# A message-passing layer on one core: picked rows put together by TensorE, slots in PSUM, ranks straight from TensorE's counts

## The chip, the cores and the metric

One of the 8 cores of a Trainium2 chip runs the whole program. The metric is the device time of one execution in microseconds (us). Engines are named as in the profile: PE (TensorE), DVE (VectorE), ACT (ScalarE), POOL (GpSimd) and SP (SyncE, which issues most DMAs).

## The reference

A graph layer over N = 6250 nodes and E = 206250 edges, 64 features, float32. The edges are sorted by their target `dst`.

```python
h = jnp.maximum(_layernorm(x, axis=-1), 0.0)
msg = jax.nn.relu(h[src] + edge_attr)
agg = jax.ops.segment_sum(msg, dst, num_segments=x.shape[0])
h = h + agg
h = jax.nn.relu(h @ W1 + b1)
out = x + h @ W2 + b2
```

So each edge needs one row of h out of 6250 (a gather by `src`), an addition of its attribute, a relu, and a sum into its target's row.

## The kernel before

**Layout.** Edges are taken in 269 groups of 768 (128 partitions x G = 6 columns; the last is short). `z` in SBUF holds h transposed and collects the sums: one-hot matmuls (`window_sum`) sum a group's messages into a window of W = 32 nodes, and DVE adds the window into `z` at the group's first node (`sum_into_z`). `slot` holds each edge's place in its window, and `one_hot` compares it with the numbers 1 to 32 (`slots`).

**Rows come in two ways.** Of each column of 128 edges the 128 rows of h are either gathered by POOL from `h_rows` in DRAM (an indirect DMA for one column, `gather`, each with a memset of the small tile `rest` behind it on POOL's queue), or picked on chip by PE. After the first F0 = 5 groups, the groups come in sets (`GROUPS`, KS = 144 sets): five of every six sets hold two groups, three columns of each gathered and three picked; the sixth holds one group, with all six columns picked. So a set has 6 or 0 gathers, and always 6 picked columns.

**Picking.** h lies in `hp` as two float16 parts, high and low, of every node. For a pair of sets (d), DVE compares node numbers with `sources` (`find`, four compares of 1536 columns, giving `found`; two ACT operations, `find_begin` and `find_beyond`, do the last 49th of the nodes) and ranks with `spots` (`back`, six compares of 1536, giving `backs`). PE multiplies `hp` by `found` (`across_of`), turns it (`turn_of`), and multiplies `picked` by `backs` into a PSUM pick bank (`pick`). The numbers that the compares look for (rank, part, spot) are worked out for 18 columns at a time in the `rank_*` steps: PE counts, before each edge, the earlier edges of the same part (`rank_count`), and DVE takes the rank out of these counts (`rank_of`).

**Decoding.** The pick bank holds for each column a high part and a low part, and a value that is one last bit smaller than its two parts say is stored negated: the value is max(b, -ONE_LESS * b) with b = high + low/FINE. In `decode(k)` ACT scales the low part (L685), DVE adds (L687), takes the maximum (L689), adds the edge attribute (L692), and adds the attributes of the gathered columns too (L695, which waits for the set's gathers). `messages` is ACT's relu (L702).

**Order.** The schedule is manual: each engine runs its instructions in the order in which the code records them. `both_units(k)` is one unit, for one set: first DVE's part (decode of set k-1, the compares for the pairs ahead, the rank steps, the one-hot of set k-1, the adds into z of set k-3), with the steps woven together by `weave`; then three stages s = 0, 1, 2 of PE and ACT: a turn, an across, in one of them the messages or the window sums of set k-2, and two of the unit's six picked columns. POOL's gathers for a set wait for picks of the set AHEAD = 9 earlier (`fetch_next`), and a ring of 11 buffers holds what they bring.

Of the kernel before, what the change touches and what calls it, by code (L numbers as in the profile page):

```python
# [68 lines left out]
BIAS, STEP = 4096, 512  # L69
# [4 lines left out]
ONE_LESS = 1 - 2.0 ** -24  # L74
# [6 lines left out]
def kernel(  # L81
# [77 lines left out]
    nc.gpsimd.iota(from0, pattern=[[1, S], [0, H]], base=0, channel_multiplier=0, allow_small_or_imprecise_dtypes=True)  # L159
# [8 lines left out]
    nc.vector.memset(ones_b, 1.0)  # L168
    upper = const.tile([P, P], F16, name="upper")
# [3 lines left out]
    for j in range(J):  # L173
        nc.gpsimd.iota(ids[j * S:(j + 1) * S], pattern=[[STEP * J, Q]], base=BIAS + STEP * j,
                       channel_multiplier=1, allow_small_or_imprecise_dtypes=True)
# [146 lines left out]
    ats, counts, marks, holds, ranks, spot_i = {}, {}, {}, {}, {}, {}  # L322
# [5 lines left out]
    def rank_count(c):  # L328
        ps = psum.tile([P, RG, PARTS, H], F32, name="rows", bufs=1)
        at = ats[c]  # L330
        nc.tensor.matmul(ps, upper, at, start=True, stop=False)
        for d in range(1, H):
            last = nc.tensor.matmul(ps[:, :, :, d:], ones_b, at[:, :, :, :H - d], start=False, stop=(d == H - 1))
# [4 lines left out]
    def rank_counted(c):  # L338
        counts[c] = rank.tile([P, RG, PARTS, H], F16, name="before", bufs=1)
        nc.scalar.copy(counts[c], made.pop(c))  # L340

    def rank_of(c):
        mine = counts.pop(c)
        nc.vector.tensor_tensor(mine, mine, ats[c], ALU.mult)
        yield
        ranks[c] = rank.tile([P, CC], F16, name="rank_of")
        with nc.allow_low_precision("a rank is a whole number below 2048"):
            nc.vector.tensor_reduce(ranks[c].rearrange("p (g j) -> p g j", j=H),
                                    mine.rearrange("p g m j -> p g j m"), AX.X, ALU.add)
# [20 lines left out]
    def rank_fits(c):  # L370
        rk = ranks.pop(c).rearrange("p (g j) -> p g j", j=H)
        pieces = ((0, 2, G - H), (2, 4, 0), (4, RG, G - H)) if c % 2 == 0 else ((0, RG, G - H),)
        for u, to, c0 in pieces:
# [5 lines left out]
            nc.vector.scalar_tensor_tensor(mine, rk[:, u:to], float(S), mine, op0=ALU.is_lt, op1=ALU.mult)  # L379
# [43 lines left out]
    pick_banks = [psum.tile([P, 2, 512], F32, name=f"pick{i}", bufs=1) for i in range(2)]  # L423
    turns = [pick_banks[0][:, 0], pick_banks[0][:, 1], half_banks[1], half_banks[2]]
    turns_made = [0]

# [49 lines left out]
    def ln_parts(r, m, h):  # L476
# [13 lines left out]
        nc.vector.tensor_tensor(hp[:, r:r + m], hp[:, r:r + m], sign.unsqueeze(2).to_broadcast([PP, m, 2, D]), ALU.mult)  # L490
# [68 lines left out]
    beyond = const.tile([P, 1], F32, name="beyond")  # L559
    nc.vector.tensor_scalar_mul(beyond, nodes_of[:, BB:], -1.0)  # L560

    def find_begin(d):
        found[d] = hot.tile([P, PARTS * BB + J, 4, S], F16, name="found")
        far = found[d][:, BB * PARTS:].rearrange("p m u s -> p (m u s)")
        nc.scalar.activation(far, sources[d][:, :J * 4 * S], AF.Abs, bias=beyond)
        return far

    def find_beyond(far):
        nc.scalar.activation(far, far, AF.Relu, bias=ones[:, 0:1], scale=-1.0)

    def find(d):
# [52 lines left out]
    def pick(k, i, t):  # L624
        d, u = k // 2, k % 2 * 2 + i
        ps = pick_banks[k % 2][:, i, :2 * H * D].rearrange("p (w t d) -> p w t d", w=2, t=H)
# [30 lines left out]
    def one_hot(gs):  # L657
        n = len(gs) * G
        g = gs[0]
        oh = work.tile([P, 2 * G, W], F32, name="oh", bufs=2)  # L660
        it = nc.vector.tensor_tensor(
            oh[:, :n], slot[:, g * G:g * G + n].unsqueeze(2).to_broadcast([P, n, W]),
            slots.unsqueeze(1).to_broadcast([P, n, W]), ALU.is_equal)
# [14 lines left out]

    def decode(k):
        ps = pick_banks[k % 2][:, :, :2 * H * D].rearrange("p i (w s) -> p i w s", w=2)  # L680
        n = len(GROUPS[k])
        ea, xg = eas[(k + RAWS) % EAS][:, :n], xgs[(k + RAWS) % RING]
        h = ps[:, :, 0]
        both = work.tile([P, 2, H * D], F32, name="both", bufs=1)
        nc.scalar.mul(both, ps[:, :, 1], 1.0 / FINE)  # L685
        yield
        nc.vector.tensor_tensor(both, h, both, ALU.add)  # L687
        yield
        nc.vector.scalar_tensor_tensor(h, both, -ONE_LESS, both, op0=ALU.mult, op1=ALU.max)  # L689
        yield  # L690
# [479 lines left out]
```

## Time and profile before

| | |
|---|---|
| time, median of 3 runs | 1239.59 us (1237.26 to 1239.94) |
| profiled execution | 1239.42 us, span 1237.4 us, mean granted clock 0.897 |
| PE, DVE, ACT, POOL busy | 918.2, 1005.9, 804.4, 1089.7 us |
| gathers and memsets on POOL | 748 each, 768.7 and 320.6 us |

A row of a group reads: line, engine, operation, out<-in, shapes, count | busy us, mean ns | idle us just before, and what ended it. A row of the timeline reads: start, us, engine, line, operation, count, and in brackets idle time before. A row of the waits reads: engine and line <- what it waited for: us in total, times, longest. A row of the stages reads: from:to, length, busy us and (count) of each engine, granted clock, DMA share, GB/s.

### The profile page before, as it was taken

How to read it: one execution, taken by the hardware profiler on the slowest of the kernel's cores; microseconds unless marked ns; L12 is line 12 of the kernel's file. 1: busy time of each engine (PE TensorE's matmuls, PEld its weight loads, DVE VectorE, ACT ScalarE, POOL GpSimd, SP SyncE). 2: the span in 40 equal slices, each digit the busy share in tenths (PEclk: the TensorE clock that was granted, in tenths of full speed). 3: DMA queues.
4: the chain of work that ended last, by engine and by line, in shares of the span. 5: the costliest groups of instructions: out<-in, count | busy, mean ns of one | idle time of the engine just before them, and what ended most of it. 6: DMA issues, size and time to landing. Idle time of an engine off the chain costs nothing. (4 is left out here: it accounts for less than half of the span.)

```text
span 1237.4 us, 37614 instructions
## 1 busy us (share of the span) xinstructions
PE 918.2 (74%) x14441; PEld 840.1 (68%) x14441; DVE 1005.9 (81%) x2286; ACT 804.4 (65%) x1605; POOL 1089.7 (88%) x1511
## 2 busy tenths in 40 slices
PE   1348888889877868858778768777886886787864
PEld 0227887778766867758767767777775785776754
DVE  8778999999887878868878877887787797786764
ACT  4438778778756757748657656676675775675642
POOL 8888988889888988988888888888888888888884
PEclk9969999999988889979889888898888988998977
DMA  6315565555554435535445445454554554454531
GB/s 194 96 41 168 168 184 156 169 174 160 152 145 147 148 107 153 154 112 166 138 143 155 135 118 147 138 159 129 147 150 134 162 150 121 135 154 123 159 73 49
DMA packets 92788, 173.63 MB, mean 140 GB/s; under 512 B 23673, under 2 KB 61178, under 8 KB 92602
## 3 DMA queue, kind: packets, MB, share of 16 engines
q1 hardware_dynamic: 68554, 146.58, 36.2%
q0 software_dynamic: 23936, 24.56, 11.3%
q8 instruction: 115, 1.88, 0.6%
q14 instruction: 71, 0.58, 0.1%
q10 hardware_dynamic: 112, 0.03, 0.0%
HBM read 167.22 MB, written 3.87 MB: 138 GB/s over the span
## 5 line engine op out<-in xcount | busy, mean ns | idle before, releaser
L225 POOL DMA_INDIRECT xg<-h_rows,src_sb x718 | 736.4, 1026 | 127.3 <-issue 77.4
L628 PE MATMUL pick<-picked,backs 128*128 128x128 f16 x5184 | 403.6, 234 | 1.2 <-DVE z L655 1.2
L622 ACT CAST picked<-half 128x512 f16<-128x512 f32 x432 | 253.2, 586 | 155.8 <-PE half L614 150.7
L628 PEld LDWEIGHTS <-backs 128*128 128x128 f16 x5184 | 338.3, 105 | 16.8 <-issue 7.1
L228 POOL MEMSET rest_of_pool<- 128x256 f16 x748 | 320.6, 429 | 0.4
L604 PE MATMUL half<-found,hp 128*128 128x128 f16 x3456 | 290.9, 232 | 27.2 <-ACT picked L622 25.8
L584 DVE TENSOR_SCALAR backs<-spots,ids 128x1536 f16<-128x1536 int16 x432 | 284.8, 686 | 0.1
L609 ACT CAST across<-half 128x512 f16<-128x512 f32 x432 | 258.3, 598 | 31.8 <-PE half L604 25.7
L604 PEld LDWEIGHTS <-hp 128*128 128x128 f16 x3456 | 240.8, 106 | 43.8 <-issue 36.6
L695 DVE SCALAR_TENSOR_TENSOR ea<-xg,ea 128x384 f32<-128x384 f32 x120 | 66.5, 554 | 158.0 <-DMA xg<-h_rows,src_sb 130.7
L574 DVE TENSOR_SCALAR found<-sources,nodes_of 128x1536 f16<-128x1536 int16 x288 | 188.3, 694 | 6.2 <-PE pick L628 4.1
L614 PE MATMUL half<-ident_h,across 128*128 128x128 f16 x1728 | 183.2, 233 | 0.8 <-ACT across L609 0.8
L702 ACT ACTIVATE ea<-ea 128x768 f32<-128x768 f32 x144 | 115.6, 803 | 100.8 <-DVE ea L695 95.6
L716 PE MATMUL pick<-oh,ea 128*64 128x32 f32 x3224 | 127.6, 229 | 8.8 <-ACT ea L702 8.8
L716 PEld LDWEIGHTS pick<-oh,ea 128*64 128x64 f32 x3224 | 111.0, 143 | 34.0 <-issue 15.7
L614 PEld LDWEIGHTS <-across 128*128 128x128 f16 x1728 | 127.9, 106 | 1.4 <-ACT across L609 1.2
L685 ACT ACTIVATE both<-pick 128x384 f32<-128x384 f32 x144 | 70.6, 490 | 50.8 <-PE pick L628 42.8
L687 DVE TENSOR_TENSOR both<-pick,both 128x384 f32<-128x384 f32 x144 | 78.1, 542 | 30.7 <-ACT both L685 29.8
L402 PE MATMUL rows<-holds,marks 128*96 128x96 f16 x288 | 28.0, 238 | 95.9 <-DVE holds L366 89.7
L384 PE MATMUL rows<-ident_b,spot_i 128*18 128x128 bf16 x48 | 11.6, 241 | 117.1 <-DVE spot_i L352 116.9
L402 PEld LDWEIGHTS <-marks 128*96 128x96 f16 x288 | 26.5, 152 | 97.1 <-DVE marks L362 77.6
L384 PEld LDWEIGHTS <-spot_i 128*18 128x18 bf16 x48 | 4.2, 88 | 125.6 <-DVE spot_i L352 124.2
(124 smaller groups left out, 914.3 us busy)
## 6 DMA issues: line engine op xcount, KB each, us to landing
sources<-source_row SPq DMA_DIRECT2D x72, 768.0 KB
ea<-in_edge_attr_dram SPq DMA_DIRECT2D x118, 384.0 KB
spots<-spot_rows SPq DMA_DIRECT2D x72, 384.0 KB
xg<-h_rows,src_sb POOLq DMA_INDIRECT x718
ea<-in_edge_attr_dram SPq DMA_DIRECT2D x32, 192.0 KB
xb<-in_x_dram SPq DMA_DIRECT2D x12, 128.0 KB
out_dram<-o SPq DMA_DIRECT2D x12, 128.0 KB
h_rows<-x SPq DMA_DIRECT2D x3, 384.0 KB
```

The source lines that it names most:

```text
L225: it = nc.gpsimd.indirect_dma_start(out=xg[:, j, :], out_offset=None, in_=rows[:, :], in_offset=bass.IndirectOffsetOnAxis(ap=idx[:, j:j + ...
L228: nc.gpsimd.memset(rest, 0.0)
L574: nc.vector.tensor_scalar(found[d][:, b * PARTS + m:b * PARTS + m + PARTS // 2].rearrange("p m u s -> p (m u s)"), sources[d][:, m * 4 * S ...
L584: nc.vector.tensor_scalar(backs[d][:, q, w].rearrange("p t s -> p (t s)"), spots[d].bitcast(I16), ids[:, w * QW + q:w * QW + q + 1], None, ...
L604: last = nc.tensor.matmul(ps[:, j * P:(j + 1) * P], hp[:, b * PARTS + m].rearrange("p t d -> p (t d)"), found[d][:, b * PARTS + m].rearran ...
L609: nc.scalar.copy(across[d, q].rearrange("p u j s -> p j u s"), ps.rearrange("p (j u s) -> p j u s", j=J, u=4))
L614: last = nc.tensor.matmul(ps[:, u * P:(u + 1) * P], ac[:, u].rearrange("p j s -> p (j s)"), ident_h, start=True, stop=True)
L622: nc.scalar.copy(picked[d][:, q].rearrange("p u d -> p (u d)"), turned.pop((d, q)))
L628: it = nc.tensor.matmul(ps[:, :, t], backs[d][:, q % QW, q // QW, u * H + t, :], picked[d][:, q, u].rearrange("p (w d) -> p w d", w=2), st ...
L687: nc.vector.tensor_tensor(both, h, both, ALU.add)
L702: nc.scalar.activation(msg, msg, AF.Relu)
L716: last = nc.tensor.matmul(pa[i * D:(i + 1) * D], msg[:, j, :], oh[:, j, :], start=(j < lo + 2), stop=(j >= G - 2))
```

## The change

1. **Decode by PE.** ACT copies a half of a pick bank to SBUF as float16 (`both`) and makes relu(-high) (`minus`); PE adds four products with scaled identities (`weigh_high`, `ident_h`, `weigh_sign`, `weigh_last`) back into the same bank; DVE then needs one addition per half, straight from PSUM. L687 and L689 go. In `ln_parts` only the high part takes the sign.
2. **Slots in PSUM.** `one_hot` reads the numbers 1 to 32 from a spare corner of a pick bank instead of SBUF.
3. **Ranks off the counts.** PE adds AMONG = 1024 where an edge has its own part (`ahead_h`), so that DVE takes the rank by a maximum straight from PSUM; the copy to SBUF (`rank_counted`, L340) and the product with `at` (L344) go. Numbers that ranks are compared with are shifted by 1024.
4. **The third compare on DVE.** `find_begin` and `find_beyond` (two ACT operations a pair, L565 and L569) become one compare of 512 columns on DVE.
5. **Pick banks own tiles**, one for each half.
6. **Order.** The decode, the one-hot and the adds into z of a unit are recorded after stage 1 (`banked_steps`), behind all compares of the unit; the messages move from stage 0 to stage 1.

POOL's gathers and memsets are the same, in the same order.

```diff
     def rank_count(c):
         ...
         nc.tensor.matmul(ps, upper, at, start=True, stop=False)
+        nc.tensor.matmul(ps, ahead_h, at, start=False, stop=False)
...
-    def rank_counted(c):
-        counts[c] = rank.tile([P, RG, PARTS, H], F16, name="before", bufs=1)
-        nc.scalar.copy(counts[c], made.pop(c))
-
     def rank_of(c):
-        mine = counts.pop(c)
-        nc.vector.tensor_tensor(mine, mine, ats[c], ALU.mult)
-        yield
...
-                                    mine.rearrange("p g m j -> p g j m"), AX.X, ALU.add)
+                                    made.pop(c).rearrange("p g m j -> p g j m"), AX.X, ALU.max)
...
-    pick_banks = [psum.tile([P, 2, 512], F32, name=f"pick{i}", bufs=1) for i in range(2)]
+    pick_banks = [[psum.tile([P, 512], F32, name=f"pick{i}{j}", bufs=1) for j in range(2)] for i in range(2)]
...
+    slots_in = [banks[0][:, 512 - W:] for banks in pick_banks]
...
-    def find_begin(d):
+    def find(d):
         found[d] = hot.tile([P, PARTS * BB + J, 4, S], F16, name="found")
-        far = found[d][:, BB * PARTS:].rearrange("p m u s -> p (m u s)")
-        nc.scalar.activation(far, sources[d][:, :J * 4 * S], AF.Abs, bias=beyond)
-        return far
-
-    def find_beyond(far):
-        nc.scalar.activation(far, far, AF.Relu, bias=ones[:, 0:1], scale=-1.0)
-
-    def find(d):
+        nc.vector.tensor_scalar(found[d][:, BB * PARTS:].rearrange("p m u s -> p (m u s)"),
+                                sources[d][:, :J * 4 * S], nodes_of[:, BB:], None, op0=ALU.is_equal)
+        yield
...
+        mine = slots if g < F0 else slots_in[set_of[g][0] % 2]
         it = nc.vector.tensor_tensor(
             oh[:, :n], slot[:, g * G:g * G + n].unsqueeze(2).to_broadcast([P, n, W]),
-            slots.unsqueeze(1).to_broadcast([P, n, W]), ALU.is_equal)
+            mine.unsqueeze(1).to_broadcast([P, n, W]), ALU.is_equal)
...
+    def decode_parts(k, i):
+        if i == 0:
+            fetched[k] = (work.tile([P, 2, 2, H * D], F16, name="both", bufs=2),
+                          work.tile([P, 2, H * D], F16, name="minus", bufs=2))
+        both, minus = fetched[k]
+        nc.scalar.copy(both[:, i], picks_of(k, i))
+        nc.scalar.activation(minus[:, i], both[:, i, 0], AF.Relu, scale=-1.0)
+
+    def decode_sum(k, i):
+        both, minus = fetched[k]
+        terms = (weigh_high, both[:, i, 0]), (ident_h, both[:, i, 1]), (weigh_sign, minus[:, i]), (weigh_last, minus[:, i])
+        for j, (weights, rows) in enumerate(terms):
+            nc.tensor.matmul(picks_of(k, i)[:, 0], weights, rows, start=(j == 0), stop=(j == len(terms) - 1))
+
     def decode(k):
...
-        both = work.tile([P, 2, H * D], F32, name="both", bufs=1)
-        nc.scalar.mul(both, ps[:, :, 1], 1.0 / FINE)
-        yield
-        nc.vector.tensor_tensor(both, h, both, ALU.add)
-        yield
-        nc.vector.scalar_tensor_tensor(h, both, -ONE_LESS, both, op0=ALU.mult, op1=ALU.max)
-        yield
...
-        nc.vector.scalar_tensor_tensor(to, h, 1.0 / UP, to, op0=ALU.mult, op1=ALU.add)
-        yield
+        for i in range(2):
+            one = to[:, i].rearrange("p j d -> p (j d)")
+            nc.vector.scalar_tensor_tensor(one, picks_of(k, i)[:, 0], 1.0 / (UP * FINE), one, op0=ALU.mult, op1=ALU.add)
+            yield
...
-    def other_steps(k):
+    def banked_steps(k):
         if k:
+            yield from decode(k - 1)
             one_hot(GROUPS[k - 1])
             yield
         if k > 1:
             yield from adds(k - 3)
+
+    def other_steps(k):
...
             for t in range(2):
                 pick(k, *divmod(2 * s + t, H))
+            if s < 2 and k:
+                decode_sum(k - 1, s)
+            if s == 1:
+                weave(banked_steps(k))
+            if s == 2:
+                decode_parts(k, 0)
```

(`decode_parts(k - 1, 1)` stands in stage 0.)

71 lines of the change are left out of this document (34 added, 37 removed).

## The prediction

> **What bounds the kernel now.** I read the page first for the engines' shares, then the groups and the source view of POOL's two lines, then the waits, then a timeline of 16 us in the middle, the stages, and last the tail.
>
> ```profile
> PE 918.2 (74%) x14441; PEld 840.1 (68%) x14441; DVE 1005.9 (81%) x2286; ACT 804.4 (65%) x1605; POOL 1089.7 (88%) x1511
> ```
>
> POOL is the busiest, at 88%. What are the other 12%?
>
> ```profile
> L225 POOL DMA_INDIRECT xg<-h_rows,src_sb x718: 949/958/1541, 50.8 to 1221.9; - x180
> L225 POOL DMA_INDIRECT xr<-in_x_dram,src_sb x18: 950/1034/1686, 3.8 to 30.7; - x18
> L228 POOL MEMSET rest_of_pool<- x748: 325/330/741, 4.9 to 1222.9; 128x256 f16 x187
> ...
> POOL xg L225 <- issue: 77.4, 453, 1.9
> POOL xg L225 <- PE pick L628: 22.5, 106, 1.9
> ...
> DVE ea L695 <- DMA xg<-h_rows,src_sb: 130.7, 49, 5.4
> ```
>
> The first three rows give minimum, median and maximum in ns and first and last start. From 3.8 to 1222.9 us POOL does 748 gathers, each with a memset behind it. The waits (total us, times, longest) show that it is never held back: 77.4 over 453 and 22.5 over 106 are about 0.17 to 0.2 us each, the gap that stands before every gather. DVE in turn waits 130.7 us for gathered rows. So POOL's own stream sets the time.
>
> ```profile
> sum 1238.00, POOL 768.67; mean POOL 51.24
> ...
> sum 1238.00, POOL 320.62; mean POOL 21.37
> ...
> 1221.90 0.95 POOL L225 DMA_INDIRECT xg<-h_rows,src_sb  x1 [0.16 <-DVE pick L689]
> 1222.85 0.33 POOL L228 MEMSET rest_of_pool<- 128x256 f16 x1
> 1224.78 0.56 DVE L695 SCALAR_TENSOR_TENSOR ea<-xg,ea 128x384 f32<-128x384 f32 x1 [2.35 <-DMA xg<-h_rows,src_sb]
> ```
>
> These are the busy sums of all gathers (768.7) and all memsets (320.6), and the tail. POOL ends at 1223.2. The profiled run's time of 1239.4 is made up so: 3.8 before the first gather; 748 x 0.950 = 710.6 of gathers at their minimum; 748 x 0.325 = 243.1 of memsets at theirs; 130.1 of gaps (1219.4 less both sums, 0.174 each); 14.2 from POOL's end to the span's; 2.0 outside the span; and **two tolls**, 768.7 - 710.6 = 58.1 us on gathers and 320.6 - 243.1 = 77.5 us on memsets. The run is 0.2 us under the median of the runs, 1239.6. Only the tolls, the start and the tail can move. Who takes the tolls?
>
> ```profile
> 602.46 0.54 DVE L661 TENSOR_TENSOR oh<-slot,slots 128x384 f32<-128x384 int16 x1
> 602.90 0.33 POOL L228 MEMSET rest_of_pool<- 128x256 f16 x1
> 602.93 0.55 DVE L689 SCALAR_TENSOR_TENSOR pick<-both 128x384 f32<-128x384 f32 x1
> ...
> 610.03 0.55 DVE L689 SCALAR_TENSOR_TENSOR pick<-both 128x384 f32<-128x384 f32 x1
> 610.26 1.15 POOL L225 DMA_INDIRECT xg<-h_rows,src_sb  x1 [0.16 <-PE pick L628]
> 612.80 1.99 DVE L584 TENSOR_SCALAR backs<-spots,ids 128x1536 f16<-128x1536 int16 x3
> 613.34 1.07 POOL L225 DMA_INDIRECT xg<-h_rows,src_sb  x1 [0.17 <-issue]
> 614.40 0.64 POOL L228 MEMSET rest_of_pool<- 128x256 f16 x1
> ```
>
> A memset that starts while DVE runs a compare (TENSOR_SCALAR, L584 or L574) takes 0.64 us; beside the two-input operations L661 and L689 it takes 0.33. A gather that starts in a compare takes 1.07, and one that starts in L689, which reads two SBUF tiles, 1.15, against 0.95. So compares toll both, by 0.31 and 0.12, and operations with two SBUF inputs toll gathers alone.
>
> **The change, part by part.** POOL's 748 gathers and memsets keep their order, so its terms change only through DVE.
>
> *DVE, removed.*
>
> ```profile
> L584 DVE TENSOR_SCALAR backs<-spots,ids 128x1536 f16<-128x1536 int16 x432 | 284.8, 686 | 0.1
> L574 DVE TENSOR_SCALAR found<-sources,nodes_of 128x1536 f16<-128x1536 int16 x288 | 188.3, 694 | 6.2 <-PE pick L628 4.1 <-DMA sources<-source_row 0.5 <-PE half L604 0.2
> L689 DVE SCALAR_TENSOR_TENSOR pick<-both 128x384 f32<-128x384 f32 x144 | 82.4, 572 | 0.0
> L692 DVE SCALAR_TENSOR_TENSOR ea<-pick,ea 128x384 f32<-128x384 f32 x144 | 78.7, 547 | 0.0
> L687 DVE TENSOR_TENSOR both<-pick,both 128x384 f32<-128x384 f32 x144 | 78.1, 542 | 30.7 <-ACT both L685 29.8 <-ACT before L340 0.9
> L661 DVE TENSOR_TENSOR oh<-slot,slots 128x192 f32<-128x192 int16 (+1 forms) x149 | 74.9, 503 | 8.7 <-PE pick L716 8.2 <-DVE ea L695 0.5
> L695 DVE SCALAR_TENSOR_TENSOR ea<-xg,ea 128x384 f32<-128x384 f32 x120 | 66.5, 554 | 158.0 <-DMA xg<-h_rows,src_sb 130.7 <-issue 26.9
> L655 DVE TENSOR_TENSOR z<-z,pick 128x32 f32 x269 | 47.8, 178 | 5.8 <-PE rows L742 2.2 <-issue 0.6 <-ACT both L685 0.3
> L366 DVE TENSOR_TENSOR holds<-rank_of,from 128x576 f16<-128x576 f16 x48 | 26.2, 545 | 0.0
> L326 DVE TENSOR_TENSOR at<-part,from_b 128x432 f16<-128x432 f16 x48 | 21.6, 451 | 0.1
> L362 DVE TENSOR_TENSOR marks<-at,node 128x432 f16<-128x432 f16 x48 | 21.6, 450 | 0.0
> L344 DVE TENSOR_TENSOR before<-before,at 128x432 f16<-128x432 f16 x48 | 18.1, 376 | 3.5 <-ACT before L340 3.5
> ```
>
> L687, L689, L692 and L344 go: 257.3 us. 288 adds of 192 columns come; 32 columns take 178 ns (L655) and 384 take 547 (L692), so 192 take about 0.35 and all of them 100 us. 72 compares of 512 columns come: between a third of L584's 0.686 and all of it, and I take 0.25, near the third since the columns are most of it, so 18 us. DVE falls by about 140 us, to 866. That alone gains nothing, since DVE waits for POOL. What counts is three effects on the tolls.
>
> (a) *Two-input operations.* The memset toll, 77.5 at 0.31 each, is 250 memsets; as many gathers at 0.12 make 30 us of the gathers' 58.1. The other 28 belong to two-input operations. Part of that lies in the prologue:
>
> ```profile
> 0.00:60.00 60.00, 38.59 (x36) 1.00 0.47 145
> ```
>
> Its 36 gathers take 1.072 each, 4.4 us over the minimum, and the normalisation that causes it stays. Of the remaining 23.6, L689 (gone), L661 (its second input now in PSUM) and L344 (gone) hold 175.4 us of busy time; L695, L366, L326 and L362, which stay, hold 135.9. By busy time 56% goes: **-13.3 us**. The ends are 0 (compares cause it all) and -28.
>
> The Trainium skill ("SBUF — State Buffer", Who interferes with whom) says that a VectorE instruction with two SBUF inputs contends with GpSimd instructions that read SBUF and not with those that only write it, which agrees with 0.33 beside L661 and L689. But it also infers that descriptor generation needs only the write interface, so that such an operation does not stall a gather; by that, (a) would be 0 and the sum 1237. The row at 610.26, 1.15 us under L689 with no compare near, speaks against it.
>
> (b) *72 more compares.* 18 us on 473.1 is 3.8%, and the compares' tolls now are 77.5 + 30 = 107.5: **+4.1 us**; with 0.69 each it would be +11.
>
> (c) *Order and density.* The compares used to alternate with decode steps; now they come in runs.
>
> DVE, one unit with six `backs` compares, before:
>
> ```order
> L584 TENSOR_SCALAR backs<-spots,ids 128x1536
> L661 TENSOR_TENSOR oh<-slot,slots 128x384
> L689 SCALAR_TENSOR_TENSOR pick_207<-both 128x2x192
> L584 TENSOR_SCALAR backs<-spots,ids 128x1536
> L655 ISA
> L655 TENSOR_TENSOR z<-z,pick_207 128x32
> L692 SCALAR_TENSOR_TENSOR ea_136<-pick_207,ea_136 128x2x192
> L584 TENSOR_SCALAR backs<-spots,ids 128x1536
> ```
>
> and such a unit after:
>
> ```order
> L578 TENSOR_SCALAR backs<-spots,ids 128x1536 x4
> L363 TENSOR_TENSOR marks_208<-at,node 128x6x72
> L578 TENSOR_SCALAR backs<-spots,ids 128x1536
> L367 TENSOR_TENSOR holds<-rank_of,from_105 128x576
> L578 TENSOR_SCALAR backs<-spots,ids 128x1536
> L380 SCALAR_TENSOR_TENSOR slot<-rank_of,slot 128x2x3
> L380 SCALAR_TENSOR_TENSOR slot<-rank_of,slot 128x6
> L380 SCALAR_TENSOR_TENSOR slot<-rank_of,slot 128x2x3
> L699 SCALAR_TENSOR_TENSOR ea_144<-pick_215,ea_144 128x192
> L699 SCALAR_TENSOR_TENSOR ea_144<-pick_216,ea_144 128x192
> L702 SCALAR_TENSOR_TENSOR ea_144<-xg_147,ea_144 128x2x192
> ```
>
> The decode moved behind all compares of its unit. Six compares in a run take twice 1.99 us; a POOL round under full toll takes 1.07 + 0.64 + 0.17 = 1.88, so the run covers 2.1 rounds and costs 2.1 x 0.43 = 0.92, or 0.15 a compare. Today it is 107.5 / 720 = 0.15. So the runs change nothing by themselves. But the stages show that a fuller DVE pays more:
>
> ```profile
> 200.00:300.00 100.00, 87.66 (x1495) 80.95 (x1493) 95.75 (x218) 79.95 (x163) 90.16 (x121) 0.96 0.56 165
> 800.00:900.00 100.00, 80.73 (x1287) 74.72 (x1286) 78.82 (x180) 68.85 (x141) 88.08 (x124) 0.90 0.49 142
> ```
>
> (busy of PE, PEld, DVE, ACT, POOL, then the clock.) From 200 to 300 DVE is 95.75% busy and POOL spends 90.16 on 60.5 pairs, 1.490 each; from 800 to 900 it is 78.8% and 88.08 on 62, 1.421. The pair's minimum is 1.275, so the tolls are 0.215 and 0.146. Some of that is denser compares: the first stage holds 218 DVE instructions against 180, 21% more, so 0.146 would be 0.177, and 0.038 is left for 17 points of DVE. DVE falls by 11 points here (140 of 1237), so by 0.025 a pair, 18 us at most; much of it is (a) again, and I take **-7 us**, with the ends +5 and -15.
>
> Sum: 1239.4 - 13.3 + 4.1 - 7 = **1223.2**.
>
> *PE.* Behind picks of a unit now stand sums of the unit before:
>
> ```order
> L622 MATMUL pick_216<-picked,backs 128x2x64
> L691 LDWEIGHTS weigh_high
> L691 MATMUL pick_218<-both,weigh_high 128x192
> L691 LDWEIGHTS ident_h
> L691 MATMUL pick_218<-both,ident_h 128x192
> L691 LDWEIGHTS weigh_sign
> L691 MATMUL pick_218<-minus,weigh_sign 128x192
> L691 LDWEIGHTS weigh_last
> L691 MATMUL pick_218<-minus,weigh_last 128x192
> L608 LDWEIGHTS across
> ```
>
> where before picks were followed by `across` at once:
>
> ```order
> L628 LDWEIGHTS backs
> L628 MATMUL pick_207<-picked,backs 128x2x64
> L614 LDWEIGHTS across
> L614 MATMUL half_206<-ident_h,across 128x128
> L614 LDWEIGHTS across
> ```
>
> 1152 matmuls of 192 columns are added.
>
> ```profile
> 601.62 0.83 PE L628 MATMUL pick<-picked,backs 128*128 128x128 f16 x12
> ```
>
> Twelve of 128 columns take 0.83 us, so 192 columns about 0.10, 119 us in all; one more rank matmul in three units adds some 11. PE rises to about 1048, 85% of the span; it was 87.7% busy in the stage 200:300. Hidden behind POOL.
>
> *ACT.*
>
> ```profile
> L685 ACT ACTIVATE both<-pick 128x384 f32<-128x384 f32 x144 | 70.6, 490 | 50.8 <-PE pick L628 42.8 <-DVE pick L689 7.3 <-issue 0.6
> L569 ACT ACTIVATE found<-found,ones 128x512 f16<-128x512 f16 x72 | 53.0, 736 | 0.1
> L565 ACT ACTIVATE found<-sources,beyond 128x512 f16<-128x512 int16 x72 | 52.6, 731 | 1.9 <-DMA sources<-source_row 1.9
> L340 ACT CAST before<-rows 128x432 f16<-128x432 f32 x48 | 24.7, 515 | 1.2 <-PE rows L333 1.2
> ```
>
> These 201 us go; 288 casts of 384 columns at 0.49 (141) and 288 of 192 columns, between 0.25 and 0.49, taken at 0.33 (95), come. ACT ends near 840, hidden too.
>
> *The new wait.* L699 waits for PE's last sum. Queued behind it on DVE are L702, the one-hot, the adds into z and the next compares; ACT's messages and PE's window sums wait for those. Its cover is the 130.7 us that DVE spends waiting for gathers, and POOL itself takes nothing from any of this until the picks of nine sets earlier are late. Without cover it is the PE rival below. The slots' copies, the scaled identities and the rank's reduction out of PSUM cost DVE under 2 us. In some units a `spots` load moves behind a store on SP's queue; it has a unit's time to land. The tail's chain (last gather, L702, message, window sum) keeps its steps: 14.2.
>
> **The rivals.** *Compares alone make the tolls* (0.11): (a) is 0, and 1239.4 + 4.1 with (c) between 0 and -7 gives 1237 to 1243, about no change. For it: the compares' 0.64 and 1.07 recur; against it the row at 610.26.
>
> *Slower: the runs lock onto POOL* (0.11). Compares will fill 491 us, 40% of POOL's time. If memset and gather starts fall into runs in proportion, 300 of 748 rounds pay 0.43, 129 us against 107.5: +21.5, without (c). With (a) that is 1248, without it 1261. It decides from about 280 tolled memsets on (250 now): 30 more at 0.43 eat up (a). For it: back-to-back compares leave no free moment inside a run. Against it: a stretch of some 2 us without compares now follows each run.
>
> *Slower: PE becomes the bound* (0.08). At 1048 us busy and a granted clock of 0.9 it fits; at 0.78, matmuls stretch to 1048 x 0.9 / 0.78 = 1209, and at 95% busy the time is about 1270. The stage 200:300, 87.7% busy at 0.96, speaks against it.
>
> **How the numbers follow.** The forecast has 0.70: 1223, on its own 1204 to 1236. The range reaches into the no-change case and the cheaper end of the locked runs: 1203 to 1246. A measurement of this kernel can tell about 0.2%, 2.5 us, from no change. Faster 0.70; same 0.11; slower 0.19.
>
> **What would show it.** Right: POOL still gapless from about 4 us to 14 us before the end; gathers' mean from 1.028 to about 1.00; memsets' at about 0.43; DVE near 866 with longer waits for gathers. Wrong: POOL waits of over 0.3 us on PE (the PE rival), a memset mean over 0.45 (locked runs), or gathers still at 1.03 (compares alone).

## The result and the profile after

The changed kernel takes **1248.97 us** (median of 5 runs, 1245.43 to 1251.39) against 1239.55 us of the kernel before (5 runs): a ratio of **1.0076, interval 1.0055 to 1.0097**. It is slower, by 9.4 us, where 16 us less were forecast. The profiled execution took 1247.1 us, 7.7 more than that of before.

The engines' line of the page of after:

```profile
PE 994.1 (80%) x15641; PEld 907.7 (73%) x15641; DVE 890.5 (72%) x2171; ACT 852.6 (68%) x1845; POOL 1097.6 (88%) x1511
```

DVE has lost 115 us, PE and ACT have gained 76 and 48, and POOL is the busiest as before, at the same 88%. Its two lines in the source view (minimum, median, maximum in ns, first and last start):

```profile
L232 POOL DMA_INDIRECT xg<-h_rows,src_sb x718: 949/952/1639, 51.6 to 1229.9; - x180
...
L232 POOL DMA_INDIRECT xr<-in_x_dram,src_sb x18: 950/1043/1754, 3.8 to 31.1; - x18
...
L235 POOL MEMSET rest_of_pool<- x748: 325/331/749, 4.9 to 1230.8; 128x256 f16 x187
```

The waits of after, then the groups:

```profile
DVE ea L702 <- DMA xg<-h_rows,src_sb: 228.0, 66, 6.9
...
PE pick L622 <- DVE z L649: 152.5, 60, 6.4
POOL xg L232 <- issue: 68.4, 417, 0.2
```

```profile
L232 POOL DMA_INDIRECT xg<-h_rows,src_sb x718 | 742.7, 1034 | 127.3 <-issue 68.4 <-PE half L608 14.4 <-PE half L598 13.2
L235 POOL MEMSET rest_of_pool<- 128x256 f16 x748 | 321.3, 430 | 0.4
L699 DVE SCALAR_TENSOR_TENSOR ea<-pick,ea 128x192 f32<-128x192 f32 x288 | 95.4, 347 | 66.5 <-PE pick L691 55.4 <-ACT ea L709 2.5 <-ACT minus L685 2.2
L563 DVE TENSOR_SCALAR found<-sources,nodes_of 128x512 f16<-128x512 int16 x72 | 30.5, 423 | 4.3 <-PE pick L622 3.9 <-DMA sources<-source_row 0.5
```

POOL still starts at 3.8 us and still waits 0.16 to 0.2 us before each gather (127.3 us over xg, to the digit as before). DVE waits 228.0 us for gathers instead of 130.7, and PE 152.5 us for DVE's additions into z, which stand behind these: what POOL brings sets the time. The sum of before, made once more:

| term of POOL's stream, us | before | after |
|---|---|---|
| start | 3.8 | 3.8 |
| 748 gathers and 748 memsets at their minimum | 953.7 | 953.7 |
| gaps | 130.1 | 130.4 |
| toll on gathers | 58.1 | **65.1** |
| toll on memsets | 77.5 | 78.2 |
| from POOL's end to the span's | 14.2 | 14.2 |

So of the 8.0 us between the two profiled spans 7.0 are a toll on gathers and 0.7 one on memsets. A count of the gathers' durations over the traces, from 105 us on, shows which ones. Before, 218 took 1.06 to 1.10 us and 20 took 1.25 us or more; after, 164 and **53**. The 33 additional long ones carry 12 us more over the minimum (19.3 against 7.4), the 54 that are fewer among those of 1.06 to 1.10 us give back 7. The 130 gathers of after beside which DVE does nothing pay 0.1 us together, so the toll comes from DVE.

What a long one looks like, in the timeline of after (start, us):

```profile
151.05 2.48 DVE L578 TENSOR_SCALAR backs<-spots,ids 128x1536 f16<-128x1536 int16 x4
151.17 1.31 POOL L232 DMA_INDIRECT xg<-h_rows,src_sb  x1 [0.16 <-issue]
152.48 0.63 POOL L235 MEMSET rest_of_pool<- 128x256 f16 x1
153.28 1.29 POOL L232 DMA_INDIRECT xg<-h_rows,src_sb  x1 [0.16 <-issue]
153.45 0.44 DVE L363 TENSOR_TENSOR marks<-at,node 128x432 f16<-128x432 f16 x1
153.81 0.63 DVE L578 TENSOR_SCALAR backs<-spots,ids 128x1536 f16<-128x1536 int16 x1
154.37 0.54 DVE L367 TENSOR_TENSOR holds<-rank_of,from 128x576 f16<-128x576 f16 x1
154.56 0.33 POOL L235 MEMSET rest_of_pool<- 128x256 f16 x1
```

The gather at 153.28 starts 0.25 us before the end of a compare (151.05 + 2.48). Behind that compare stands a rank step of 0.44 us and then another compare, and the gather takes 1.29 us where the prediction's row for a gather in a compare had 1.07. But the gather at 151.17, which lies in the unbroken run of four compares, takes 1.31 as well, so the step in between is not the only way to a long one. Before, a decode step stood at such a place (L687, one SBUF input), and the rank steps came behind all compares.

### The profile page after: what moved, and what is told of

The parts are those of the page before. It is cut to its first block, busy times and chain, and to the rows that moved or that the text cites. A ratio compares the mean times of both kernels' runs of the same rounds, so it can differ in the third digit from the quotient of the medians.

```text
span 1245.4 us, 39974 instructions
## 1 busy us (share of the span) xinstructions
PE 994.1 (80%) x15641; PEld 907.7 (73%) x15641; DVE 890.5 (72%) x2171; ACT 852.6 (68%) x1845; POOL 1097.6 (88%) x1511
## 4 chain that ended last, share of the span: by engine, by line
PE 47%; POOL 16%; DMA 14%; DVE 6%; issue 5%; ACT 3%; DVEq 1%; POOLq 0%; ACTq 0%
PE pick L622 17%; DMA xg<-h_rows,src_sb 14%; POOL xg L232 11%; PE half L598 9%; PE pick L691 6%; PE pick L723 5%; PE half L608 5%; POOL rest_of_pool L235 5%; DVE oh L656 2%; DVE found L568 1%; ACT ea L709 1%; PE half L593 1%; ACT source L412 1%; PE rows L403 1%; PE rows L749 1%
## 5 line engine op out<-in xcount | busy, mean ns | idle before, releaser
L232 POOL DMA_INDIRECT xg<-h_rows,src_sb x718 | 742.7, 1034 | 127.3 <-issue 68.4
L622 PE MATMUL pick<-picked,backs 128*128 128x128 f16 x5184 | 385.8, 227 | 152.6 <-DVE z L649 152.5
L622 PEld LDWEIGHTS <-backs 128*128 128x128 f16 x5184 | 325.0, 102 | 171.8 <-issue 162.6
L235 POOL MEMSET rest_of_pool<- 128x256 f16 x748 | 321.3, 430 | 0.4
L598 PE MATMUL half<-found,hp 128*128 128x128 f16 x3456 | 277.3, 226 | 1.0 <-DVE found L568 0.9
L702 DVE SCALAR_TENSOR_TENSOR ea<-xg,ea 128x384 f32<-128x384 f32 x120 | 66.9, 558 | 243.6 <-DMA xg<-h_rows,src_sb 228.0
L598 PEld LDWEIGHTS <-hp 128*128 128x128 f16 x3456 | 227.2, 102 | 15.2 <-issue 9.1
L684 ACT CAST both<-pick 128x384 f16<-128x384 f32 x288 | 141.9, 493 | 21.3 <-PE pick L723 18.4
L699 DVE SCALAR_TENSOR_TENSOR ea<-pick,ea 128x192 f32<-128x192 f32 x288 | 95.4, 347 | 66.5 <-PE pick L691 55.4
L723 PEld LDWEIGHTS pick<-oh,ea 128*64 128x64 f32 x3224 | 107.0, 138 | 32.2 <-issue 14.5
L723 PE MATMUL pick<-oh,ea 128*64 128x32 f32 x3224 | 123.6, 225 | 7.7 <-ACT ea L709 7.7
L685 ACT ACTIVATE minus<-both 128x192 f16<-128x192 f16 x288 | 104.5, 363 | 9.2
L691 PE MATMUL pick<-both,weigh_high 128*128 128x192 f16 x288 | 75.3, 262 | 0.2 <-ACT both L684 0.2
L691 PE MATMUL pick<-both,ident_h 128*128 128x192 f16 x288 | 75.2, 261 | 0.0
L691 PE MATMUL pick<-minus,weigh_sign 128*128 128x192 f16 x288 | 75.0, 260 | 0.1
```

Source lines behind the costliest of these rows:

```text
L232: it = nc.gpsimd.indirect_dma_start(out=xg[:, j, :], out_offset=None, in_=rows[:, :], in_offset=bass.IndirectOffsetOnAxis(ap=idx[:, j:j + ...
L235: nc.gpsimd.memset(rest, 0.0)
L598: last = nc.tensor.matmul(ps[:, j * P:(j + 1) * P], hp[:, b * PARTS + m].rearrange("p t d -> p (t d)"), found[d][:, b * PARTS + m].rearran ...
L622: it = nc.tensor.matmul(ps[:, :, t], backs[d][:, q % QW, q // QW, u * H + t, :], picked[d][:, q, u].rearrange("p (w d) -> p w d", w=2), st ...
L684: nc.scalar.copy(both[:, i], picks_of(k, i))
L691: nc.tensor.matmul(picks_of(k, i)[:, 0], weights, rows, start=(j == 0), stop=(j == len(terms) - 1))
```

## Experiments

The theories. **A**: the prediction's account, tolls by the piece, from compares and from two-input steps. **C**: the 72 added compares make the loss. **D**: the order on DVE makes it, the rank steps between compares above all. **PE**: PE's own pace. Ratios are to the kernel before on the same chip. That matters here: on the chips of the result and of the first eight runs below, before takes 1238 to 1240 us ("the first kind of chip"); on those of all others, from found_twice on, 1254 to 1256 ("the second kind").

### slots_sbuf: the one-hot's second input back in SBUF

```diff
-        mine = slots if g < F0 else slots_in[set_of[g][0] % 2]
+        mine = slots
```

> The changed kernel with one edit: the one-hot reads the numbers 1 to 32 from SBUF again, so 144 operations of 0.51 us have two SBUF inputs again. Theory A (two-input operations toll gathers by their share, as the prediction had it): the gathers' toll grows by 74 / 311 of 23.6 us, some 5 to 6 us; time 1254. Theory B (the compares and their place make the toll, two-input operations little): within 3 us of the changed kernel, 1246 to 1252, gathers' mean within 5 ns of 1.037 us.

Measured: 1251.75 us, 1.0102 [1.0083, 1.0121]. That is 0.0026 over after, 3 us, with overlapping intervals; gathers 785.8 us in all (after 775.7), memsets 316.5 (321.3). It has the sign that A gives it, but memsets gave back half of what gathers lost.

### far_on_act: the third compare back on ACT

```diff
-        nc.vector.tensor_scalar(found[d][:, BB * PARTS:]..., sources[d][:, :J * 4 * S], nodes_of[:, BB:], None, op0=ALU.is_equal)
+        nc.scalar.activation(far, sources[d][:, :J * 4 * S], AF.Abs, bias=beyond)
+        nc.scalar.activation(far, far, AF.Relu, bias=ones[:, 0:1], scale=-1.0)
```

> The changed kernel with the compare for the nodes beyond the 48th part back on ACT (two operations a pair of sets), so 72 of the 792 compares leave DVE. Theory C (the added compares cost it): they took 30.5 us of DVE; 3.8 to 6% of the tolls of some 107 us goes, 4 to 7 us; time 1242 to 1245, about half of the loss. Theory D (the order of the compares costs it, not their number): under 2 us, 1247 to 1251.

Measured: 1246.72 us, 1.0065 [1.0051, 1.0079]. Taking 72 compares away gives 1.4 us by the ratio, within the uncertainty; the 4 to 7 us of C did not come back.

### ranks_last: the rank steps behind the compares

```diff
-        weave(compared, counted_by_columns(k), others)
+        weave(compared)
+        weave(counted_by_columns(k), others)
```

> The changed kernel with the rank steps recorded behind all compares of their unit instead of between the last of them; same operations, another order. Theory D (gathers of 1.25 us and over, 53 after against 20 before, come from compares that stand with a rank step between them): most of these are rank units, so the class falls by half and the time by 5 to 10 us, to 1239 to 1244. Theory C (number of compares): no change, 1247 to 1251.

Measured: 1242.54 us, 1.0036 [1.0020, 1.0052], and 26 gathers of 1.25 us or more instead of 53. The place of a few steps of some 0.5 us alone is worth 5 us, about half the loss.

### before_runs: before's operations, six compares in an unbroken run

```diff
-        for _ in range(3):
+        for _ in range(6):
             next(compared, None)
         for _ in range(3):
             next(decoded, None)
-            next(compared, None)
             next(others, None)
```

> The kernel before with one edit: the compares of a unit are recorded in one run ahead of the decode steps instead of between them. Theory D (order): the loss of the change shows without the rest of it, 1244 to 1252 with gathers' mean from 1.028 to 1.035 us or more. The prediction's step (c) (a run costs what the same compares cost apart): 1237 to 1242.

Measured: 1238.46 us, 0.9998 [0.9985, 1.0012]. A run without anything in it costs nothing, as the prediction said (rival "locked runs": no). Its tolls changed all the same, 64.2 and 71.0 us against 58.1 and 77.5: what gathers lost, memsets gave back.

### ranks_between: before's operations in an order like after's

```diff
         for _ in range(3):
-            next(decoded, None)
-            next(compared, None)
             next(others, None)
...
-        weave(decoded, compared, counted_by_columns(k), others)
+        weave(compared, counted_by_columns(k), others)
+        weave(decoded)
```

> The kernel before, all its operations as they are, with the order of after: the compares from the fourth on woven with the rank steps, and the decode behind the compares. If the order alone makes the loss: the count of gathers of 1.25 us or more goes from 20 to 45 or more and the ratio is 1.004 to 1.009, POOL still without waits. Rival: the order costs nothing on these operations (the loss needs the decode from PSUM or the missing L687 and L689): ratio 0.999 to 1.002, count near 20.

Measured: 1257.86 us, **1.0152 [1.0132, 1.0172]**, 19 us. Nothing but the order differs from before. POOL's groups, and a place in its timeline:

```profile
L225 POOL DMA_INDIRECT xg<-h_rows,src_sb x718 | 754.8, 1051 | 127.3 <-issue 76.3 <-PE pick L628 17.8 <-PE half L604 10.4
L228 POOL MEMSET rest_of_pool<- 128x256 f16 x748 | 320.7, 429 | 0.4
```

```profile
160.48 0.86 DVE L584 TENSOR_SCALAR backs<-spots,ids 128x1536 f16<-128x1536 int16 x1
160.60 0.33 POOL L228 MEMSET rest_of_pool<- 128x256 f16 x1
161.09 1.30 POOL L225 DMA_INDIRECT xg<-h_rows,src_sb  x1 [0.17 <-PE half L604]
161.26 0.44 DVE L362 TENSOR_TENSOR marks<-at,node 128x432 f16<-128x432 f16 x1
161.62 0.64 DVE L584 TENSOR_SCALAR backs<-spots,ids 128x1536 f16<-128x1536 int16 x1
```

The same gaps, the same memsets, and 18.4 us more on the gathers xg (736.4 before). The long gather is the one seen in after, 1.30 us with marks between two compares; but 29 of the 51 gathers of 1.25 us or more have no rank step beside them. That the order alone costs time is shown, on operations that the change did not touch; how much of it is the rank steps is counted below.

### ranks_far: both repairs together

> After's kernel with both changes: the rank steps behind the compares, and the third compare back on ACT. If the two gains add (ranks_last 1.0036, far_on_act 0.0011 below after): 1.0025, with 1.001 to 1.004. If the rank order and the compares' number act on the same gathers, 1.0036 as with ranks_last alone. Rival: what remains of the loss lies with the added 72 compares once the order is mended: then 1.000 or less.

(The edits of ranks_last and far_on_act.) Measured: 1246.40 us, 1.0059 [1.0044, 1.0074]: above ranks_last (the intervals overlap), although 72 compares are gone. All three expectations missed. The gains of the single edits did not add.

### steps_twice and steps_twice_last: marks and holds issued twice

```diff
+        for _ in range(2):
             nc.vector.tensor_tensor(marks[c][:, :, :PARTS], at, over(node[:, c], PARTS), ALU.mult)
...
+        for _ in range(2):
             it = nc.vector.tensor_tensor(holds[c], over(ranks[c], S), in_all(from0, S), ALU.is_equal)
```

> After's kernel with L363 (marks) and L367 (holds) each issued twice, back to back, in their places: 96 more short two-input steps, some 48 us of DVE, half of them in sets with six compares standing between two compares. Theory order, narrow (a pause of 0.44 us between two compares is what lets the second compare meet a gather before its second access): the pause becomes about 0.9 us and the count of gathers of 1.25 us or more falls below 53; the ratio is between 1.004 and 1.009. Theory order, wide (any two-input step between compares lengthens the gathers that meet it): the count rises to 65 to 90, ratio 1.010 to 1.017. Rival, load (only the busy time of two-input steps counts, not their place): 48 us at the 5 us per 75 us of the slots run is +3 us, ratio 1.010, and the same +3 us with the steps behind the compares.

> The same doubled steps, but behind the compares (the order of ranks_last, 1.0036). Theories of order, narrow and wide: the added steps no longer stand between compares, so only the load is left: 1.004 to 1.007, and the count of gathers of 1.25 us or more stays near the 26 of that order. Rival, load: 1.006, and steps_twice no more than 0.004 above it, as in the pair without doubling.

Measured: 1243.82 us, 1.0052 [1.0032, 1.0071], and with the order of ranks_last 1239.71 us, 1.0009 [0.9996, 1.0021]. Both medians are *below* those without the doubled steps (1.0076 and 1.0036; the intervals overlap, by a hair in the second pair), the second below all that was expected, with DVE at 931.9 and 942.6 us busy. POOL's groups in steps_twice:

```profile
L232 POOL DMA_INDIRECT xg<-h_rows,src_sb x718 | 752.5, 1048 | 127.8 <-issue 70.6 <-PE pick L625 17.3 <-PE half L611 11.9
L235 POOL MEMSET rest_of_pool<- 128x256 f16 x748 | 306.3, 409 | 0.4
```

Gathers lost 10 us more and memsets won 15. The ratio fell into what the narrow theory of order gave, but not for its reason: 52 gathers of 1.25 us or more are left, against 53. The load theory (+3 us) is wrong in sign. By the piece, as A prices them, 96 additional two-input steps make a kernel slower.

### found_twice: 288 compares issued twice

```diff
                 nc.vector.tensor_scalar(found[d][:, b * PARTS + m:...], sources[d][:, m * 4 * S:...], nodes_of[:, b:b + 1], None, op0=ALU.is_equal)
+                nc.vector.tensor_scalar(found[d][:, b * PARTS + m:...], sources[d][:, m * 4 * S:...], nodes_of[:, b:b + 1], None, op0=ALU.is_equal)
```

> The changed kernel with each of the 288 found compares of 1536 columns issued twice, same result; DVE gets 190 us more, to about 1080 of 1250. Theory A (each compare holds up POOL, 0.15 us a compare): 288 x 0.15 = 43 us more, 1280 to 1300. Theory D (the order makes the toll, the number of compares little): under 15 us more, 1250 to 1264.

Measured, on the second kind of chip: 1313.83 us, 1.0479 [1.0454, 1.0503]. POOL stays without gaps:

```profile
L232 POOL DMA_INDIRECT xg<-h_rows,src_sb x718 | 788.6, 1098 | 127.0 <-issue 62.2 <-PE pick L626 19.5 <-PE half L612 13.2
L235 POOL MEMSET rest_of_pool<- 128x256 f16 x748 | 335.4, 448 | 0.4
```

45.9 and 14.1 us more than in after: 60 us for 288 compares, 0.21 each where A has 0.15. After was profiled on the first kind of chip, though, where before itself has 11 us less of tolls (before_again, below); without these it is 0.17. So compares do hold POOL up, and one more of them back to back costs about what A has. Of the 156 gathers of 1.25 us or more in this run 48 lie beside compares alone. This is a sum of durations on POOL; the ratio itself tells nothing, since after alone has the same on such a chip (after_again, below).

### before_no_memset and after_no_memset: the 748 memsets left out

```diff
-            nc.gpsimd.memset(rest, 0.0)
```

> The kernel before without the memset behind each gather. Theory A (POOL's stream sets the time): POOL's 748 rounds lose the memset, 320.6 us, and the next bound takes over: DVE, which did a unit in about 6.9 us in the stage 200:300 where it was 95.75% busy; 144 x 6.9 and some 120 us of start and tail give 1100 to 1130. Theory PE (PE and its waits set the time): no more than 20 us gained.

> The changed kernel without the memset behind each gather. Theory A: with POOL out of the way the change shows what it took from DVE; the stage 130:200 of the changed kernel, where PE was 98.8% busy, did a unit in about 6.1 us; 144 x 6.1 and 120 us give 990 to 1040, 7 to 11% under the kernel before without memsets. Theory PE (its sums and waits make the changed kernel slower by themselves): at or above the kernel before without memsets.

Measured: 1307.97 us, 1.0422 [1.0399, 1.0444], and 1315.95 us, 1.0499 [1.0474, 1.0524]. Both are slower, where 243 us of memsets and all their tolls were gone. A's 1100 to 1130 and 990 to 1040 us were missed by far; theory PE, with no more than 20 us gained, holds, though it named no loss. The waits of before_no_memset:

```profile
POOL xg L225 <- PE pick L627: 182.2, 169, 13.6
...
POOL xg L225 <- issue: 96.2, 315, 0.5
```

POOL has caught up with its pacing (the picks of nine sets earlier), so PE sets the time. Some 180 of PE's 300 us of idle time there are "issue", with nothing that it waits for; why PE is slower so than when POOL paces it, the profile does not say.

### woven: the decode between the next unit's compares

```diff
-        weave(compared, counted_by_columns(k), others)
+        weave(compared, banked, counted_by_columns(k), others)
...
-            if s == 1:
-                weave(banked_steps(k))
```

(`banked` is the unit before's banked_steps; in this order part of the sums is not the reference's.)

> The changed kernel with the decode, the one-hot and the adds of a unit recorded between the compares of the next unit, as the kernel before had them, instead of behind stage 1. Theory D (the loss comes from the order on DVE): back to the kernel before or under it, 1230 to 1242. Theory PE (PE then waits for DVE's decode ahead of each unit's picks): slower than the changed kernel, 1255 or more. Theory of the added compares: 1246 to 1251.

Measured: 1427.24 us, 1.1347 [1.1314, 1.1381]. POOL waits 180.8 us for picks, PE for the adds into z, and DVE's addition L702 for gathers: a ring of waits, not tolls. It says nothing on D.

### alternate and alternate_first: after's operations in before's alternation

```diff
-        weave(compared, counted_by_columns(k), others)
+        weave(counted_by_columns(k), others)
...
-                weave(banked_steps(k))
+                weave(banked_steps(k), compared)
```

> After's operations in before's alternation: three compares, the rank steps, then L699, compare, L699, compare, L702, compare, one-hot, adds. If the order makes the whole loss, the ratio is 0.990 to 1.000 (before's tolls with the two-input steps gone; 0.987 if the prediction's sum held for all the rest), with fewer than 30 gathers of 1.25 us or more. Rival, the operations lose as well (the added compares, the sums behind PE): 1.003 to 1.008 as with ranks_last. DVE's L699 waits for PE here with compares queued behind it, as before's decode did for ACT.

> As alternate, with the rank steps ahead of the first compare instead of behind the third. If what stands between compares counts, this is at or below alternate, by 0 to 0.005. If only the moment counts at which compares start against POOL's stream, it can differ from alternate by up to 0.005 to either side.

(In alternate_first the rank steps stand ahead of the first compare.) Measured, on the second kind of chip: 1269.91 us, 1.0101 [1.0072, 1.0130], and 1261.72 us, 1.0058 [1.0036, 1.0080]. The first was wanted at or below 1.000, so on such a chip the order is not all. But after itself has 1.047 there, and with the alternation POOL is the bound again (88%, gaps as before): the order is worth 4% where PE is slower. The tolls did not go back to before's: gathers pay 95.8 and 86.4 us over their minimum here, against 64.9 in before_again.

### padded, padded_again, after_again and before_again

```diff
+            nc.vector.tensor_copy(pad, slots)
+            nc.vector.tensor_copy(pad, slots)
```

(behind each L702; the other two are the kernels as they are.)

> After's kernel with two copies of 32 columns (one SBUF input, some 0.2 us together) behind each of the 120 additions L702: no step between compares, no two-input step added, 25 us of DVE. If what stands between compares counts, nothing changes: 1.0076, within 0.002, and 45 to 60 gathers of 1.25 us or more. If the moment counts at which DVE's steps start against POOL's stream, since the chain behind L702 starts with a landed gather and keeps its phase: the gathers that start under the one-hot or the next compare change class, and the ratio moves by 0.003 or more to either side.

> After's kernel as it is. If its loss is one of POOL's tolls alone, 1.005 to 1.010 on any chip, with POOL without gaps and 45 to 60 gathers of 1.25 us or more. If the chip's PE pace counts, on a chip where the kernel before takes 1254 us the ratio is 1.015 or more, with waits of POOL for PE of over 0.3 us; on one where it takes 1238 us, 1.005 to 1.010.

> The padded kernel once more. On a chip where the kernel before takes about 1238 us: if the copies themselves bring PE's own pace to the fore, again 1.04 or more; if the chip does, 1.005 to 1.012. On one where it takes 1254 us, 1.047 again under both.

> The kernel before as it is, for its profile on this chip: POOL without gaps and the tolls of 58 and 78 us on a chip with 1238 us; on one with 1254 us some 15 us more, in the gathers' and memsets' durations if the tolls differ, in POOL's idle time if PE's pace does.

Measured, on the second kind of chip: padded 1316.19 us, 1.0474 [1.0448, 1.0500], and again 1315.83, 1.0485 [1.0455, 1.0516]; **after_again 1312.38 us, 1.0470 [1.0438, 1.0503]**; before_again one run, 1257.3 us. So the copies cost nothing, and padded told nothing of the moment at which steps start: PE was the bound. The chain of waits by engine, of after:

```profile
PE 47%; POOL 16%; DMA 14%; DVE 6%; issue 5%; ACT 3%; DVEq 1%; POOLq 0%; ACTq 0%
```

and of after_again, with its rows of POOL's end, of the groups and of the waits:

```profile
PE 70%; issue 12%; ACT 10%; DVE 0%; another core or an unknown queue 0%; DMA 0%; DVEq 0%; ACTq 0%
```

```profile
L235 POOL MEMSET rest_of_pool<- x748: 325/330/746, 4.9 to 1246.9; 128x256 f16 x187
```

```profile
L232 POOL DMA_INDIRECT xg<-h_rows,src_sb x718 | 735.0, 1024 | 158.6 <-PE pick L622 52.2 <-issue 45.7 <-PE half L608 19.5
L235 POOL MEMSET rest_of_pool<- 128x256 f16 x748 | 312.5, 418 | 0.4
```

```profile
PE pick L723 <- issue: 62.7, 137, 1.6
...
PE pick L622 <- issue: 36.0, 109, 0.5
```

There POOL is *less* tolled than on the first kind (127.6 us in all against 143.3) and done at 1247.2, but the span ends at 1304.6: PE is behind. Its clock was granted at 0.917, as in after (0.922). What differs is idle time between its instructions that nothing in the profile explains ("issue"), 62.7 and 36.0 us ahead of L723 and L622 alone, where after has next to none, and a busy time that is 72 us longer (1066.3 against 994.1 us), although one matmul of L622 takes 231 ns on average against 227: they overlap less. PE's waits for other engines are shorter in turn.

## Why the prediction was wrong, step by step

**The bound and the sum** held. In all ten profiles on the first kind of chip, the span less the busy time of xg and of the memsets is 179.9 to 182.3 us (1245.4 - 742.7 - 321.3 = 181.4 in after; 1255.9 - 754.8 - 320.7 = 180.4 in ranks_between). Only the tolls moved the time, as the prediction said.

**The step that failed is (c)**, order and density: taken at -7 us with ends at +5 and -15. On before's operations an order like after's costs 19 us (ranks_between). It failed in two places. First, that a run of six costs 0.15 a compare as now, so that the runs change nothing by themselves, came out for unbroken runs (before_runs, 0.9998), but the order that the prediction itself quotes is not unbroken: marks and holds stand between the last compares. Those rows were read as a run. Second, "a fuller DVE pays more" was read off two stages of one profile. The windows of after (PE, PEld, DVE, ACT, POOL):

```profile
200.00:300.00 100.00, 89.21 (x1493) 82.02 (x1491) 78.44 (x188) 79.13 (x175) 90.15 (x121) 0.97 0.52 158
```

DVE is at 78.44 there instead of 95.75, and POOL spends 90.15 us on 60.5 pairs, 1.490 each, to the digit what it was. A DVE emptier by 17 points bought nothing; with the doubled steps a fuller DVE was no slower.

Where the toll went, counted over the traces: what the gathers from 105 us on take over 0.95 us, by DVE's steps that run during them (us in all):

| DVE's steps during the gather | before | after | ranks_last | ranks_between |
|---|---|---|---|---|
| no compare | 7.8 | 0.5 | 3.6 | 7.1 |
| compares alone | 8.7 | 14.3 | 19.5 | 9.6 |
| a compare and a rank step | 8.3 | **21.4** | 7.8 | **20.0** |
| a compare and other steps | 25.9 | 20.2 | 21.4 | 31.6 |
| sum | 50.7 | 56.4 | 52.3 | 68.3 |

(Rank steps here are the DVE steps at, before, rank_of, spot_i, marks, holds and slot.) So the gain that (a) hoped for is partly there, in the first row, and gathers that meet a compare and a rank step take 13 us more and eat it up. The count says what stood beside a gather, not which step held it.

**(a), two-input operations, -13.3.** Not shown as a price. The row that it rests on, 1.15 us under L689, is one of two kinds: in before, with no compare near, 13 gathers that start 0.22 us behind the start of L689 take 1.15 us, and 22 that start 0.02 or 0.03 us behind it take 0.95 to 0.97. The slots' part, by its share of busy time 74.9 / 311.3 x 23.6 = 5.7 us, was measured at 3 us with overlapping intervals; 96 additional two-input steps, by the same price 3.6 us slower, left the kernel some 3 us faster by the ratio. In the few cases beside the one-hot with no compare near, the operand makes no difference at like moments: where the one-hot begins 0.17 to 0.26 us behind the gather's start, the gather takes 1.09 and 1.13 us in after (slots in PSUM) and 1.08, 1.14 and 1.17 in slots_sbuf; where it begins 0.38 us behind or later, 0.95 in both. The Trainium skill ("SBUF — State Buffer", Who interferes with whom) infers that such operations do not stall descriptor generation. By that both edits would have changed nothing on gathers. The gathers' 785.8 us in slots_sbuf and 785.6 in steps_twice, against 775.7, can't settle it, since edits that add no such step move this sum too; but a gather of before_runs that takes 1.24 us beside L695, marks and holds, without a compare (shown below), does not agree with it. That (1.0152 - 1.0076) x 1238.5 = 9.4 us lie between ranks_between and after, close to the -9.2 of (a) and (b), is no proof: the two orders differ in the place of the one-hot and the adds, and on the second kind of chip after's operations in before's alternation are slower than before.

**(b), 72 compares, +4.1.** Each takes 0.423 us, not 0.25: 512 columns cost well over a third of 1536, and the nearer row was the whole compare. A price can't be given: taking them away gave 1.4 us in one order and lost about 3 in another, both within overlapping intervals.

**PE, ACT, DVE:** 994, 853 and 891 us against 1048, 840 and 866 forecast; hidden, on this chip.

**The rivals.** "Locked runs" has fallen: memsets' tolls hardly moved (77.5 to 78.2), and unbroken runs are free. Of "compares alone" the time has fallen, about no change; its premise has too, since gathers are held up without a compare, but what grew is on gathers that meet one. "PE becomes the bound" (0.08, 1270 us) is what happens on the second kind of chip, at 1312 us; but it does not need the low clock that the prediction made its condition. There it came with the unexplained gaps between PE's instructions.

**The moment.** Two places with the same DVE steps and no compare show why prices by the piece fail, the first in before, the second in before_runs:

```profile
241.59 0.54 DVE L695 SCALAR_TENSOR_TENSOR ea<-xg,ea 128x384 f32<-128x384 f32 x1
241.99 0.97 POOL L225 DMA_INDIRECT xg<-h_rows,src_sb  x1 [0.16 <-issue]
242.06 0.45 DVE L362 TENSOR_TENSOR marks<-at,node 128x432 f16<-128x432 f16 x1
```

```profile
242.66 0.55 DVE L695 SCALAR_TENSOR_TENSOR ea<-xg,ea 128x384 f32<-128x384 f32 x1
242.81 1.24 POOL L225 DMA_INDIRECT xg<-h_rows,src_sb  x1 [0.17 <-issue]
243.13 0.45 DVE L362 TENSOR_TENSOR marks<-at,node 128x432 f16<-128x432 f16 x1
```

Where marks starts 0.07 us behind the gather, the gather takes 0.97 us; where it starts 0.32 us behind, 1.24; and in before_runs, where it starts 0.52 us behind (the gather at 223.00), 0.95. So two-input steps do hold up a gather, by nothing or by 0.29 us, as the moment has it.

**What stays open.** The total of the tolls hangs on such moments, and every edit shifts them for all that follows; a rule that gives the total from the order was not found. That a gather takes 1.07 us in an unbroken run of compares and 1.30 only with a short step between two of them is no such rule: the gather at 151.17 of after does not fit. How the 9.4 us divide between the rank steps' place (5 us came back in ranks_last) and the place of the decode was not measured. No version beat the kernel before.

## What to carry to other kernels

When a stream without gaps is the bound and only small contention tolls can change, price the order first: write out what stands next to what at the places in question, and profile the order alone before adding up operations by the piece. Doubling or removing a suspect is no test if it shifts everything behind it, so compare sums on the bound engine over the whole run, sorted by what stands beside each piece. And a margin on the next engine (PE at 80%) is a margin on one chip only.

## What the runs showed of the hardware

- With no operation of POOL changed, memsets took between 306.3 and 325.1 us and all gathers between 768.7 and 787.1 (first kind of chip). In some edits one gave back what the other lost (before_runs, steps_twice), in ranks_between not.
- A gather beside the same DVE steps, without a compare, took 0.95, 0.97 or 1.24 us, as one of them (marks) began 0.52, 0.07 or 0.32 us behind its start; beside an idle DVE it took 0.95.
- The same program takes 1238 us on some chips and 1254 to 1256 on others. Before_again shows where: tolls of 64.9 and 81.8 us instead of 58.1 and 77.5, and 21.3 us instead of 14.2 from POOL's end to the span's. A change that costs 0.8% on the one kind costs 4.7% on the other.
- Taking 748 memsets off the busiest engine made the kernel 4.2% slower on the second kind of chip.
